# Projecting Q and K in chunks of eight heads with 26 block products

## The chip, the cores and the metric

The kernel runs on one core of a Trainium2 chip. Its time is the device time of one execution in microseconds (us); several runs are made, and their median is given. One more execution is recorded by the hardware profiler. Its instructions span a little less than its device time.

## The reference

All arithmetic is in 32-bit floats. x has 2 sequences of 512 tokens with 512 features.

```python
x = x + layernorm(attention(layernorm(x)))
x = x + layernorm(ffn(layernorm(x)))
```

The attention has 32 heads of 128, so Wq, Wk and Wv are 512 x 4096:

```python
q = rms_norm(h @ Wq + bq, gq)      # the mean square runs over all 4096
k = rms_norm(h @ Wk + bk, gk)
v = h @ Wv + bv
attn = softmax(q_head @ k_head.T / sqrt(128))
out = concat(attn @ v_head) @ Wo + bo
```

The ffn adds a base product, 512 x 512, to a gated sum of eight experts of rank 16.

## The kernel before, in words

**Stages.** The tokens of the first sequence are normalised and transposed (xTs), Q is projected, then K, then the first quarter of V. A loop over 64 pairs (head, sequence) follows, numbered i, in which scores, softmax and the weighted sum are done, with the other three quarters of V and the output projection woven in. The residual and the ffn come last.

**Projection.** `project` (line 199) goes through Q and then K in chunks of four heads (GH). Weights and tokens are split in 2 x 2 blocks and multiplied by seven block products in place of eight (Winograd's form of Strassen's scheme). For that `weight_sums` (line 188) makes four sums of weight blocks per chunk on POOL, and `token_sums` (line 177) makes four sums of token blocks once, on DVE. One block product (line 219) is, for each of two heads j, two matmuls of 128x128 weights by 128x512 tokens, added up in one PSUM bank: 28 matmuls per chunk, 16 chunks in all. DVE joins the products as they come (lines 255 to 306): one operand of nearly every join is in PSUM. ACT squares each finished head (line 240) and POOL adds the squares to accq or acck (line 241), from which the mean square comes: `ssq` for q (line 415) and `ssk` for k (line 423), both matmuls in the order of TensorE. Each head is stored in DRAM (keptq, keptk).

**Side work.** In the q stage POOL also makes the weight sums for V (`value_sums`, line 327) and DVE those for the output projection (`output_sums`, line 353); both are stored in DRAM. In the k stage DVE multiplies the stored q heads by the norm's factors: `scalings` (line 373) loads four heads at a time and stores them as keptqs, two per call of `between` (line 385).

**Value stage and head loop.** `values` (line 438) does V by the same seven products; the first 28 of its steps run ahead of the loop, each two matmuls into one of three "aux" banks. Their weights circulate in three buffers of the pool `hpool`, loaded two products ahead. `key_scales` (line 420) stands behind the third and fifth of these steps. In the loop `fetch` loads q and k three turns ahead, `scores` (line 528) multiplies them, ACT copies them out (line 535), `top_of` (line 538) takes the maximum on DVE and POOL (lines 544 to 547), DVE subtracts it (line 580), ACT takes the exponential (line 583) and TensorE multiplies by the values (line 592). Output products (line 649) are added in SBUF by DMAs that POOL issues (line 656).

**What sets the order.** TensorE (PE), VectorE (DVE), ScalarE (ACT) and GpSimd (POOL) run their instructions in the order of the program text. A framework adds the waits and gives out the buffers of each pool. SyncE (SP) issues nearly all DMAs; its order is the framework's, by when buffers come free and then by place in the text.

```python
IN_ORDER = {ET.PE, ET.DVE, ET.Activation, ET.Pool}
BANKS = (("ps", ("ps", "ps", "ps")), ("o", ("aux", "aux")), ("aux", ("ps", "aux", "aux")))
```

Of the kernel before, what the change touches and what calls it, by code (L numbers as in the profile page):

```python
# [9 lines left out]
F32 = mybir.dt.float32  # L10
# [18 lines left out]
RMS_EPS = 1e-6  # L29


@with_exitstack
def kernel(ctx: ExitStack, tc: tile.TileContext, x, wq, wk, wv, wo, vecs, rows, wbase, gates, bexp, out):
# [17 lines left out]
    npool = ctx.enter_context(tc.tile_pool(name="npool", bufs=B * NK))  # L51
    ypool = ctx.enter_context(tc.tile_pool(name="ypool", bufs=6))
    upool = ctx.enter_context(tc.tile_pool(name="upool", bufs=7))
    vpool = ctx.enter_context(tc.tile_pool(name="vpool", bufs=4))
    qpool = ctx.enter_context(tc.tile_pool(name="qpool", bufs=5))
    kpool = ctx.enter_context(tc.tile_pool(name="kpool", bufs=5))
    opool = ctx.enter_context(tc.tile_pool(name="opool", bufs=16))
    spool = ctx.enter_context(tc.tile_pool(name="spool", bufs=3))
    tmp = ctx.enter_context(tc.tile_pool(name="tmp", bufs=4))
    wpool = ctx.enter_context(tc.tile_pool(name="wpool", bufs=2))  # L60
# [8 lines left out]

    def wide(name):  # L70
        return spool.tile([P, NT, 512], F32, tag="wide", name=name)
# [17 lines left out]
    def load_w(src, name):  # L89

        w = wpool.tile([P, 4, 512], F32, tag="w", name=name)
        nc.sync.dma_start(out=w, in_=src.rearrange("(c p) f -> p c f", p=P))
        return w

# [9 lines left out]
    wq0 = load_w(wq[:, ts(0, GH * P)], "w_q0")  # L104
# [50 lines left out]
    def norm_transposed(tiles, name, tag):  # L155

        n = wide(f"n_{name}")
        pss = [pt(f"nt_{name}_{c}", tag) for c in range(NK)]
        for i, rs, shift in norms(tiles, name):
            nc.scalar.activation(n[:, i, :], tiles[i], AF.Identity, bias=shift, scale=rs)  # L160
            for c in range(NK):
                nc.tensor.transpose(pss[c][:, ts(i, P)], n[:, i, ts(c, P)], ident)

        def tiles_of():
            outs = []
            for c in range(NK):
                o = npool.tile([P, 512], F32, tag="nT", name=f"nT_{name}_{c}")
                if c % 2 == 0:
                    nc.vector.tensor_copy(o, pss[c])
                else:  # L170
                    nc.scalar.copy(o, pss[c])
                outs.append(o)
            return outs

        return tiles_of

    def token_sums(xTs):

        (b11, b21), (b12, b22) = ((xT[0:2], xT[2:4]) for xT in xTs)
        t1, t2, t3, t4 = (xpool.tile([P, 2, 512], F32, tag="x", name=f"t{i + 1}") for i in range(4))  # L180
        for c in range(2):
            nc.vector.tensor_tensor(t1[:, c], b12[c], b11[c], ALU.subtract)
            nc.vector.tensor_tensor(t2[:, c], b22[c], t1[:, c], ALU.subtract)
            nc.vector.tensor_tensor(t3[:, c], b22[c], b12[c], ALU.subtract)
            nc.vector.tensor_tensor(t4[:, c], b21[c], t2[:, c], ALU.subtract)
        return [[t[:, c] for c in range(2)] for t in (t1, t2, t3, t4)]

    def weight_sums(w, name):

        a11, a12, a21, a22 = w[:, 0:2, 0:256], w[:, 2:4, 0:256], w[:, 0:2, 256:512], w[:, 2:4, 256:512]  # L190
        pairs = [vpool.tile([P, 4, 256], F32, tag="v", name=f"s{i}_{name}") for i in range(2)]
        s1, s2, s3, s4 = out = [t[:, i : i + 2] for t in pairs for i in (0, 2)]
        nc.gpsimd.tensor_tensor(s1, a21, a22, ALU.add)
        nc.gpsimd.tensor_tensor(s2, s1, a11, ALU.subtract)
        nc.gpsimd.tensor_tensor(s3, a11, a21, ALU.subtract)
        nc.gpsimd.tensor_tensor(s4, a12, s2, ALU.subtract)
        return [a11, a12, a22] + out

    def project(xTs, sums, w_src, bias, step, name, pools, keep, accs, parts, between=lambda: None):

        G = H // GH
        begun = set()
        parts = {0: parts}
        opened = {}  # L210
        two = range(2)

        def load_next(g):
            if g < G:
                parts[g] = weight_sums(load_w(w_src[:, ts(g, GH * P)], f"w_{name}{g}"), f"{name}{g}")

        def product(g, i, a, x, j, tag=None):
            ps = pt(f"p{i}_{name}{g}_{j}", tag)
            for c in range(2):
                nc.tensor.matmul(ps, a[:, c, ts(j, P)], x[c], start=(c == 0), stop=(c == 1))  # L220
            return ps

        def column(v, g, j):
            return v[:, g * GH + j : g * GH + j + 1]

        def tile_of(what, g, j):
            return opool.tile([P, 512], F32, tag="o", name=f"{what}_{name}{g}_{j}")

        def head(g, b, j):
            pool, tag = pools[j // 2 if len(pools) > 1 else 0]  # L230
            return pool.tile([P, 512], F32, tag=tag, name=f"{name}{b}_{g * GH + j}")

        def keep_it(o, g, b, j):
            h = g * GH + j
            if b not in begun:
                begun.add(b)
                nc.scalar.activation(accs[b], o, AF.Square)
            else:
                sq = tt(f"sq_{name}{b}_{h}")
                nc.scalar.activation(sq, o, AF.Square)  # L240
                nc.gpsimd.tensor_tensor(accs[b], accs[b], sq, ALU.add)  # L241
            nc.sync.dma_start(out=keep[b, h], in_=o)

        def open_chunk(g, tag=None):
            a11, a12 = parts[g][0:2]
            ps1 = [product(g, 1, a11, xTs[0][0:2], j, tag) for j in two]
            ps2 = [product(g, 2, a12, xTs[0][2:4], j, tag) for j in two]
            u1 = opened[g] = [tile_of("u1", g, j) for j in two]

            def leave():  # L250
                for j in two:
                    nc.scalar.activation(u1[j], ps1[j], AF.Identity, bias=column(bias, g, j), scale=1.0)
                for j in two:
                    o = head(g, 0, j)
                    nc.vector.tensor_tensor(o, ps2[j], u1[j], ALU.add)
                    keep_it(o, g, 0, j)

            return leave

        if len(xTs) < B:  # L260
            load_next(1)
            leave = open_chunk(0, "ps")
            second = norm_transposed(xs[1], "a1", "aux")
            leave()
            xTs.append(second())
            leave = open_chunk(1, "ps")
            sums.extend(token_sums(xTs))
            leave()
        t1, t2, t3, t4 = sums
        for g in range(G):  # L270
            if g + 1 not in parts:
                load_next(g + 1)
            a11, a12, a22, s1, s2, s3, s4 = parts.pop(g)
            if g not in opened:
                parts[g] = (a11, a12)
                open_chunk(g)()
                del parts[g]
            u1 = opened.pop(g)
            between()
            u2 = [tile_of("u2", g, j) for j in two]  # L280
            for j in two:
                ps = product(g, 6, s2, t2, j)
                nc.vector.tensor_tensor(u2[j], ps, u1[j], ALU.add)
            between()
            u3 = [tile_of("u3", g, j) for j in two]
            for j in two:
                ps = product(g, 7, s3, t3, j)
                nc.vector.scalar_tensor_tensor(u3[j], ps, column(step, g, j), u2[j], ALU.add, ALU.add)
            between()
            for j in two:  # L290
                ps = product(g, 4, a22, t4, j)
                o = head(g, 0, j + 2)
                nc.vector.tensor_tensor(o, ps, u3[j], ALU.add)  # L293
                keep_it(o, g, 0, j + 2)
            between()
            for j in two:
                ps = product(g, 5, s1, t1, j)
                o = head(g, 1, j + 2)
                nc.vector.tensor_tensor(o, ps, u3[j], ALU.add)
                nc.vector.tensor_tensor(u2[j], ps, u2[j], ALU.add)  # L300
                keep_it(o, g, 1, j + 2)
            between()
            for j in two:
                ps = product(g, 3, s4, xTs[1][2:4], j)
                o = head(g, 1, j)
                nc.vector.tensor_tensor(o, ps, u2[j], ALU.add)
                keep_it(o, g, 1, j)
            yield g

    def attention():  # L310
# [16 lines left out]
        def value_sums(p, c):  # L327
# [10 lines left out]
            for i, w in enumerate((s1, s2, s3, s4)):  # L338
                nc.sync.dma_start(out=keptw[p, i, c], in_=w)
# [648 lines left out]
```

## Time and profile before

| what | value |
|---|---|
| median of three runs (lowest, highest) | 1307.57 us (1306.94, 1312.16) |
| the profiled execution | 1305.06 us |
| its span, first to last instruction | 1303.3 us |
| q projection's first matmul, k's, value stage's | 11.6, 205.7, 401.2 us |
| POOL's additions of squares, q and k (line 241) | 62 + 62, 81.3 + 85.5 us busy |
| scaling of q (line 385) | 64, 64.1 us busy, 1042 ns mean |
| stores of keptq, keptk, keptqs | 64 each, 256 KB, 6.4 to 6.7 us to landing |
| HBM read, written | 149.26 MB, 84.93 MB |

In the profile a group is a line of the kernel with its engine, its operation and its tiles, written out<-in; `x` counts instructions. A matmul of 32-bit floats shows as two instructions. PEld is the loading of weights, which runs beside PE. The busy time of an engine in a stretch is followed by its count; the last three numbers of such a row are the granted TensorE clock (1.00 is full), the busy share of the DMA engines and GB/s. A bracket at the end of a row tells how long the engine was idle before it and what released it.

### The profile page before, as it was taken

How to read it: one execution, taken by the hardware profiler on the slowest of the kernel's cores; microseconds unless marked ns; L12 is line 12 of the kernel's file. 1: busy time of each engine (PE TensorE's matmuls, PEld its weight loads, DVE VectorE, ACT ScalarE, POOL GpSimd, SP SyncE). 2: the span in 40 equal slices, each digit the busy share in tenths (PEclk: the TensorE clock that was granted, in tenths of full speed). 3: DMA queues.
4: the chain of work that ended last, by engine and by line, in shares of the span. 5: the costliest groups of instructions: out<-in, count | busy, mean ns of one | idle time of the engine just before them, and what ended most of it. 6: DMA issues, size and time to landing. Idle time of an engine off the chain costs nothing.

```text
span 1303.3 us, 11742 instructions
## 1 busy us (share of the span) xinstructions
PE 1279.0 (98%) x3518; PEld 652.2 (50%) x3518; DVE 977.8 (75%) x1208; ACT 541.8 (42%) x746; POOL 496.9 (38%) x382
## 2 busy tenths in 40 slices
PE   7999999999999999999999999999999999999997
PEld 4444444444444444455555555555555655555453
DVE  7565665877656468888787877778787888888976
ACT  5222222322221153445445454554545555565353
POOL 4789897555764011111121322223232232333102
PEclk9999999999999999999999999999999999999999
DMA  8789978699998765534356566566566555643301
GB/s 292 254 321 314 337 275 309 229 330 323 307 326 286 255 199 187 176 131 130 114 168 178 139 196 166 141 183 173 157 175 172 134 156 139 164 108 84 85 14 65
DMA packets 150335, 257.01 MB, mean 197 GB/s; under 512 B 12160, under 2 KB 41728, under 8 KB 150272
## 3 DMA queue, kind: packets, MB, share of 16 engines
q1 hardware_dynamic: 137312, 232.67, 52.7%
q0 software_dynamic: 12096, 22.03, 10.3%
q10 hardware_dynamic: 864, 1.57, 0.3%
q8 instruction: 28, 0.46, 0.1%
q14 instruction: 35, 0.29, 0.1%
HBM read 149.26 MB, written 84.93 MB: 180 GB/s over the span
## 4 chain that ended last, share of the span: by engine, by line
PE 68%; DVE 2%; ACT 1%; issue 0%; ACTq 0%
PE ps L534 17%; PE o L592 17%; PE aux L463 15%; PE aux L649 12%; PE psy L695 2%; PE p_k L220 2%; PE f L867 1%; PE hg L860 1%; ACT s L583 1%; PE f L923 1%; PE aux L566 0%; ACT n_f L160 0%; DVE quarters L553 0%; DVE y L830 0%; PE ssk L423 0%
## 5 line engine op out<-in xcount | busy, mean ns | idle before, releaser
L547 POOL PARTITION_ALL_REDUCE top<-m x64 | 122.2, 1910 | 606.0 <-DVE m L545 606.0
L535 ACT ACTIVATE s<-ps,rk 128x512 f32<-128x512 f32 x256 | 175.8, 687 | 308.6 <-PE ps L534 287.4
L592 PE MATMUL o<-s,v 128*128 128x512 f32 x512 | 230.6, 593 | 3.4 <-ACT s L583 3.4
L534 PE MATMUL ps<-qh,kh 128*128 128x512 f32 x512 | 230.2, 592 | 0.0
L534 PEld LDWEIGHTS ps<-qh,kh 128*128 128x128 f32 x512 | 97.3, 190 | 122.5 <-issue 120.5
L592 PEld LDWEIGHTS o<-s,v 128*128 128x128 f32 x512 | 97.0, 190 | 103.8 <-issue 95.7
L553 DVE TRANSPOSE_TENSOR_REDUCE quarters<-s 128x64 f32<-128x2048 f32 x64 | 147.2, 2300 | 0.0
L580 DVE TENSOR_TENSOR s<-s,top 128x2048 f32<-128x2048 f32 x64 | 146.0, 2282 | 0.0
L544 DVE TENSOR_TENSOR m<-s 128x1024 f32<-128x1024 f32 x64 | 78.0, 1219 | 62.0 <-ACT s L535 62.0
L583 ACT ACTIVATE s<-s 128x2048 f32<-128x2048 f32 x64 | 121.7, 1901 | 5.0 <-DVE s L580 5.0
L463 PE MATMUL aux<-w_v,t 128*128 128x512 f32 x256 | 115.8, 596 | 0.0
L649 PE MATMUL aux<-wr,oh 128*128 128x256 f32 x448 | 103.0, 380 | 0.0
L649 PEld LDWEIGHTS aux<-wr,oh 128*128 128x128 f32 x448 | 84.6, 190 | 23.2 <-issue 13.2
L241 POOL TENSOR_TENSOR accq<-accq,sq_q 128x512 f32<-128x512 f32 x62 | 81.3, 1313 | 34.6 <-ACT sq_q L240 33.0
L240 ACT ACTIVATE sq_k<-k 128x512 f32<-128x512 f32 x62 | 38.7, 630 | 133.9 <-DVE k L293 63.3
L240 ACT ACTIVATE sq_q<-q 128x512 f32<-128x512 f32 x62 | 38.9, 630 | 133.1 <-DVE q L293 68.3
L241 POOL TENSOR_TENSOR acck<-acck,sq_k 128x512 f32<-128x512 f32 x62 | 85.5, 1383 | 20.5 <-ACT sq_k L240 17.4
L463 PE MATMUL aux<-w_v,nT_a 128*128 128x512 f32 x192 | 87.5, 596 | 0.0
L220 PE MATMUL p_q<-t,s_q 128*128 128x512 f32 x192 | 85.0, 592 | 0.0
L220 PE MATMUL p_k<-t,s_k 128*128 128x512 f32 x192 | 85.0, 592 | 0.0
L649 PE MATMUL aux<-wr,s_o 128*128 128x256 f32 x336 | 77.4, 380 | 0.0
L463 PEld LDWEIGHTS aux<-w_v,t 128*128 128x128 f32 x256 | 47.6, 190 | 55.0 <-issue 54.0
(185 smaller groups left out, 1703.1 us busy)
## 6 DMA issues: line engine op xcount, KB each, us to landing
keptq<-q SPq DMA_DIRECT2D x64, 256.0 KB, 6.4
q<-keptq SPq DMA_DIRECT2D x16, 1024.0 KB, 6.6
keptk<-k SPq DMA_DIRECT2D x64, 256.0 KB, 6.6
w_v<-keptw SPq DMA_DIRECT2D x32, 512.0 KB, 4.0
keptqs<-q SPq DMA_DIRECT2D x64, 256.0 KB, 6.7
qh<-keptqs SPq DMA_DIRECT2D x64, 256.0 KB, 2.9
kh<-keptk SPq DMA_DIRECT2D x64, 256.0 KB, 2.7
keptv<-o_v SPq DMA_DIRECT2D x64, 256.0 KB, 3.0
```

The source lines that it names most:

```text
L220: nc.tensor.matmul(ps, a[:, c, ts(j, P)], x[c], start=(c == 0), stop=(c == 1))
L241: nc.gpsimd.tensor_tensor(accs[b], accs[b], sq, ALU.add)
L463: nc.tensor.matmul(ps, x[c][:, ts(t, P)], w[:, c, :], start=(c == 0), stop=(c == 1))
L534: nc.tensor.matmul(ps, kk[i][:, ts(k, P)], qs[i], start=True, stop=True)
L535: nc.scalar.activation(s[:, k, :], ps, AF.Copy, scale=rks[b][:, k : k + 1])
L544: nc.vector.tensor_tensor(m, s[:, 0:2, :], s[:, 2:4, :], ALU.max)
L547: nc.gpsimd.partition_all_reduce(ms[i], m[:, 0, :], P, ReduceOp.max)
L553: nc.vector.tensor_reduce(quarters.rearrange("p k j -> p (k j)"), ss[i].rearrange("p k (j r) -> p (k j) r", r=32), AX.X, ALU.add, apply_tr ...
L580: nc.vector.tensor_tensor(s, s, top.unsqueeze(1).to_broadcast([P, NT, 512]), ALU.subtract)
L583: nc.scalar.activation(ss[i], ss[i], AF.Exp)
L592: nc.tensor.matmul(po, vs[b, c][:, k, ts(j, P)], ss[i][:, k, :], start=(k == 0), stop=(k == NT - 1))
L649: nc.tensor.matmul(ps[:, t, :], a, right_of[i, g][:, j, :], start=(j == 0), stop=(j == 1))
```

## The change

The first two q chunks (eight heads) keep the seven products. The other 24 q heads and all k heads are done in seven chunks of eight heads. A chunk's weights are 4 x 2 blocks of 256 x 256 and the tokens 2 x 4 blocks of 256; tables written into the kernel list 26 block products (`PRODUCTS`) where two chunks of before took 14 of twice the size, 18 sums of weight blocks per chunk (`W_SUMS`), 19 sums of token blocks made once (`X_SUMS`, on DVE), and 25 joins. A product is four matmuls of 128x128 weights by 128x256 tokens. Products are added up in PSUM in eight chains of two to four products, and two stand alone: a chain's bank is copied out by ACT (`COPIES`, 16) or read by a join while the chain goes on. `JOINS` lists the 25 joins on DVE; in 15 of them both operands are in SBUF. `STEPS` gives each step a time in units of one product, and an agenda puts the steps of all chunks, side work too, in one order by these times. Of the 18 weight sums POOL makes 13 ("w") and DVE 5 ("v").

A chunk's output block is two heads by 256 tokens, so ACT adds nine biases in halves and POOL adds each square in two halves of 128x256. Seven PSUM banks circulate, an eighth is for ssq. Weights are loaded in blocks of 256 KB, eight products ahead.

Side work: the output sums 0 to 4 lie in the q chunks; the value sums of the first three quarters lie in the k chunks and are DVE's now; output sums 5 and 6 and the last value sums lie behind value steps 1 to 20, with group 6 in the two buffers of `hpool` ("h"). Of q, the heads of the first 52 turns are scaled in the loop, two turns ahead, directly in front of `top_of`, and are fetched from keptq; the last 12 are scaled in the k chunks and stored. The buffers of the q and k stage are given back at its end and used again by the later pools. The memory for DMAs that POOL issues is set to 8192.

```diff
+SCALED = 52
+PRODUCTS = (
+    (25, 21, 5, 25), (15, 2, 2, 15), (11, 9, 3, 11), (24, 18, 14, 24), (3, 16, 21, 25), (7, 11, 25, 7),
...
+STEPS = (
+    (-8.07, "w", 9), (-6.54, "w", 16), (-5.78, "w", 21), (-4.19, "v", 18), (-2.28, "w", 11), (0.0, "p", 25), (1.0, "p", 15),
+    (1.36, "c", 25), (2.0, "p", 11), (2.34, "w", 15), (2.88, "c", 15), (3.0, "p", 24), (3.23, "c", 11), (3.87, "w", 10),
...
+    (27.57, "a", 33), (27.94, "q", 47), (29.1, "a", 47), (29.58, "q", 39), (31.39, "a", 39),
+)
...
+            def product(self, k):
+                (w, x), root = operands[k], chain_of[k]
+                begun = root in self.banks
+                if not begun:
+                    self.banks[root] = free_banks.pop(0)
+                ps, a, moving = self.banks[root], self.a[w], block_of_x(x)
+                for j in range(2):
+                    for c in range(2):
+                        nc.tensor.matmul(
+                            ps[:, j, :], a[:, c, ts(j, P)], moving[:, c, :],
+                            start=(j == c == 0 and not begun), stop=(c == 1), skip_group_check=True,
+                        )
...
+            def join(self, v):
+                sign, y, z = joins[v]
...
+                nc.vector.tensor_tensor(to, y[0], z[0], ALU.add if sign > 0 else ALU.subtract)
...
+            def square(self, v):
...
+                nc.sync.dma_start(out=self.kept[n // 2, n % 2, self.h0 // 2 + i], in_=o)
+                sq = self.squared[v] = tt(f"sq_{self.name}{self.h0}_{v}").rearrange("p (j f) -> p j f", j=2)
+                nc.scalar.activation(sq, o, AF.Square)
+
+            def accumulate(self, v):
+                _, n = outputs[v]
+                acc = self.accs[n // 2][:, n % 2, :]
+                for j in range(2):
+                    nc.gpsimd.tensor_tensor(acc, acc, self.squared[v][:, j, :], ALU.add)
...
+        for n, sums_of in enumerate(X_SUMS):
+            agenda.add(-9.5 + 0.6 * n, lambda s=sums_of: x_sum(*s))
+        for g in range(5):
+            of = OutputSums(g)
+            agenda.add(16 * g - 13, of.load)
+            for n in range(4):
+                agenda.add(16 * g + 4 * n - 1.5, lambda of=of, n=n: of.step(n))
...
+        for b in range(B):
+            agenda.add(KB + 8.5 + b, lambda b=b: begin_rq(b))
...
         for n in range(28):
             next(v_steps)()
+            if n >= 1 and extra:
+                extra.pop(0)()
             if n in (2, 4):
                 key_scales(n // 2 - 1)
             if n == 12:
                 for i in range(3):
                     fetch(i)
+            if n in (16, 17):
+                scale(n - 16)
...
+            if i + 2 < N:
+                scale(i + 2)
             top_of(i + 1)
...
-    nc = bacc.Bacc("TRN2", target_bir_lowering=False, num_devices=1)
+    nc = bacc.Bacc("TRN2", target_bir_lowering=False, num_devices=1, dynamic_dma_scratch_size=8192)
```

The letters of `STEPS`: p product, c copy, j join, w and v weight sum on POOL and DVE, q bias, store and square, a addition of the square.

## Prediction

> **What bounds the kernel now.** First the page: busy shares and the chain that ended last.
>
> ```profile
> span 1303.3 us, 11742 instructions
> ...
> PE 1279.0 (98%) x3518; PEld 652.2 (50%) x3518; DVE 977.8 (75%) x1208; ACT 541.8 (42%) x746; POOL 496.9 (38%) x382
> ...
> PE 68%; DVE 2%; ACT 1%; issue 0%; ACTq 0%
> ```
>
> TensorE is never free and the chain runs over it. A share of the whole span says nothing of the stage that changes, so next the busy time by stage; the rows are the q projection, the k projection and the end of the head loop, the columns PE, PEld, DVE, ACT, POOL.
>
> ```profile
> 27.20:205.70 178.50, 178.50 (x417) 79.03 (x416) 105.74 (x138) 45.91 (x73) 151.13 (x115) 1.00 0.85 291
> 205.70:401.30 195.60, 194.80 (x455) 86.11 (x454) 141.80 (x180) 49.72 (x81) 126.16 (x92) 1.00 0.88 306
> ...
> 1010.00:1213.00 203.00, 198.93 (x619) 115.25 (x618) 177.56 (x167) 116.96 (x150) 66.34 (x55) 1.00 0.52 129
> ```
>
> PE is full at granted clock 1.00; but POOL is second in the q projection at 85% (151.13 of 178.50), and it is POOL that the change leans on. Third, prices, from the chain in order of time (start, us, piece) and from the timelines of DVE and POOL around 66 us.
>
> ```profile
> 466.64 3.43 PE ps L534 x8
> ...
> 563.67 3.45 PE aux L649 x16
> ```
>
> ```profile
> 62.81 0.81 DVE L357 TENSOR_TENSOR wo<-wo 128x512 f32<-128x512 f32 x1
> 63.66 1.64 DVE L358 TENSOR_TENSOR wo<-wo,wo 128x512 f32<-128x512 f32 x1
> 65.34 1.64 DVE L359 TENSOR_TENSOR wo<-wo,wo 128x512 f32<-128x512 f32 x1
> 67.01 1.63 DVE L360 TENSOR_TENSOR wo<-wo 128x512 f32<-128x512 f32 x1
> 68.57 1.28 DVE L255 TENSOR_TENSOR q<-p_q,u_q 128x512 f32<-128x512 f32 x2
> ```
>
> ```profile
> 57.89 8.54 POOL L241 TENSOR_TENSOR accq<-accq,sq_q 128x512 f32<-128x512 f32 x6
> 66.39 1.71 POOL L334 TENSOR_TENSOR a_v<-a_v,a_v 128x512 f32<-128x512 f32 x1
> 68.17 1.60 POOL L335 TENSOR_TENSOR s_v<-a_v,a_v 128x512 f32<-128x512 f32 x1
> 69.74 1.26 POOL L336 TENSOR_TENSOR a_v<-a_v,a_v 128x512 f32<-128x512 f32 x1
> 70.97 1.26 POOL L337 TENSOR_TENSOR a_v<-a_v,s_v 128x512 f32<-128x512 f32 x1
> ```
>
> Read: a matmul of the code is two instructions, so 512 columns cost 2 x 3.43/8 = 0.858 us and 256 columns 2 x 3.45/16 = 0.431, exactly half. A POOL addition of 128x512 steps by 1.23 us when alone (69.74 to 70.97). While DVE works on two SBUF operands the POOL steps are 1.78 and 1.57, and the DVE instruction takes 1.64 where one with a PSUM operand, beside the same busy POOL, takes 0.69 (line 283: 0.68 to 0.69). So the two slow each other, by 0.34 to 0.55 us of POOL for each such DVE instruction; I take 0.45.
>
> **Matmuls.** Removed: 6 q chunks and 8 k chunks of 28 matmuls, 392 x 0.858 = 336.1 us; they fill 62.2 to 401.3 (339.1 us) but for 1.7 of the norm's product and 1.3 idle. Added: 7 chunks of 26 x 4 = 104 matmuls of 256 columns, 728 x 0.431 = 314.0, a chunk of 44.85 us, a product 1.725. On the path: **-22 us**, if nothing else is late.
>
> **ACT**, a chunk: 16 copies (5 in two halves), 16 squares, 9 biases in two halves: 55 instructions. At the full-size step of 0.60 each, 33 us, at half of it for the halves 24; either lies beside 44.85. Off the path.
>
> **POOL**, a chunk: 13 weight sums x 1.23 = 16.0, and 32 additions of 128x256, which the trace does not show. Half of the full step is 0.61, the whole of it 1.23. In the contended stretch a POOL and a DVE instruction share 1.67 us (63.66 to 65.34), of which DVE's step is 0.60; so 1.07 is the part of POOL that scales, 0.16 fixed, and the half is 0.69. I take 0.69; 1.23 would need all cost to be fixed, against which stands a memset of 128x1 at 0.10. Sum 16.0 + 22.1 = 38.1 of 44.85, 85%.
>
> **DVE**, a chunk: 25 joins, 15 of them with both operands in SBUF (their products were copied first), 5 weight sums, and 6.7 output sums (q) or 6 value sums and 3 early scalings (k), which are all of the two-SBUF kind: 27 to 29, where the q chunks of before had 8 for eight heads. Over the stage 7 x 20 + 20 + 24 + 12 = 196, and 19 sums of x ahead: 215. Uncontended DVE has (10 + 29) x 0.6 = 23 of 44.85, contended 10 x 0.6 + 29 x 1.64 = 54. With 0.85 of them meeting POOL at work they cost POOL 215 x 0.85 x 0.45 = 82 us.
>
> POOL's queue up to the last addition of k's squares is thus 7 x 38.1 = 267, 7 for six old additions that fall in the lead, 82: 356. It starts 8.07 products (13.9 us) ahead of the first product, so it ends at 342 after it. What waits: the ssk products (line 423), which stand in PE's queue after three value steps (PE 406.32 now, 344 after the start of the stage). Net **-2 us** for the stage, in place of -22. If POOL kept up, PE would be through at 314 + 1.7, and the last addition is due 6.2 products (10.6 us) after the last product: ssk at 326, **-18**; behind it all value products wait. If all 215 collide at 0.55, POOL needs 378: **+34**. These are the ends.
>
> [...]
>
> **Start.** The sixth product needs the 17th sum of x, due 5 products (8.6 us) after the start, DVE starting 16.4 ahead: 17 x 0.6 to 1.64 = 10 to 28, with 8 exits x 0.6 and three other sums 17 to 38 in 25 us: 0 to +13, I take +2 as POOL has gaps there.
>
> **Value steps.** The sums for output group 6 move behind value step 11 and use two of the three "h" buffers in which value weights circulate. The two loads stand ahead of the weights for step 16 in order of priority; these then get a buffer only as step 15 ends, and land 4.0 us after issue ("w_v<-keptw", DMA issues), so PE waits about 4; the weights of step 18 find one buffer free and wait 4 again: **+8** (0 if the loads are ordered behind, 12 at 6 us each). The first value exits stand behind the last chunk's squares on ACT, which end about 5.7 us after the last product when uncontended; three banks cover 5.2: 0.5, inside the wait for ssk. The new sums on DVE (16 x 0.6 to 1.6) lie beside 54 us in which DVE works 24.
>
> **Head loop.** 50 scalings of 0.74 us (line 385, uncontended median 0.744) move to DVE's queue ahead of the maximum. DVE has 201 of 253 us in 757 to 1010, and waits 3.6 to 4.1 there for scores: nothing. From 1010 on:
>
> ```profile
> 1041.99 1.22 DVE L544 TENSOR_TENSOR m<-s 128x1024 f32<-128x1024 f32 x1
> ...
> 1046.37 2.28 DVE L580 TENSOR_TENSOR s<-s,top 128x2048 f32<-128x2048 f32 x1
> 1050.02 1.22 DVE L544 TENSOR_TENSOR m<-s 128x1024 f32<-128x1024 f32 x1 [1.38 <-ACT s L535]
> ```
>
> One scaling fits in the 1.38; the other pushes the subtraction's end from 1048.65 to 1049.4, and the exponential starts at 1049.89 anyway. Six heads fall here before the early-scaled ones: +0.5, at most 6 x 0.74 = 4.4. What waits behind it is the maximum, then POOL and exponentials. Gone are the k stage's 64 scalings with their 64 stores and 16 loads of 1 MB: DMA at 0.88 falls, which no wait of PE pays for. The 1 KB pieces in which heads are now fetched land three heads (30 us) ahead against 2.9 us: nothing. The memory for POOL's own DMAs is halved; the trace does not show its filling. POOL issues one or two of them per head of 10 us or more and they land in 4.5 us, so I take 0; a wait for one landing would hold the next maximum by up to 4.5 us, of which 1.2 (1048.65 to 1049.89) is covered.
>
> **Sum.** -2 + 2 + 8 + 0.5 = +8.5 on 1303.3; with 1.8 outside the span 1313.6 against the profiled 1305.06. The median of the runs is 1307.57, 2.5 above that one: **1316**.
>
> **Rivals.** *PE stays the bound* (POOL's halves at 0.61, few collisions as it has gaps): -18 + 1 + 8 = -9, 1298; without the buffer stall 1290. For it: POOL at 85% ran beside a full PE in the q stage; against: there DVE sent it 4 colliding instructions per 24 us, now 27 per 45. It decides as soon as POOL's chunk is under 44.85, i.e. fewer than 15 collisions per chunk. *POOL and DVE hold each other* (all collide, joins at 1.64 free the banks late): 215 x 0.45 makes POOL 357, +13, with 12 + 5 + 3 around it +33: 1340. For it: 54 us of contended DVE work; against: ten joins and the gaps. *The change does less than it says*: the first two q chunks keep the 28 matmuls, as counted, and 256-column matmuls might not sustain 0.2156 behind a 190 ns weight load; the 16-instruction pieces do, so I give this no time.
>
> **Chances.** 0.52 for the POOL-bound case (1303 to 1330, its middle 1316), 0.28 for PE-bound (1288 to 1299), 0.20 for the mutual hold (1325 to 1345). A measurement here tells 0.5% from no change, 1301 and 1314: faster 0.31 (the second case and a little of the first), slower 0.51 (three fifths of the first, all of the third), same 0.18. Range 1288 to 1338, leaving out the tails of the outer cases.
>
> **What would show it.** POOL-bound: POOL over 95% busy between the first product and the value stage, PE waits there released by POOL's weight sums, POOL's joint step above 1.5 us, the ssk product released by the last addition, one or two 4 us gaps of PE on "w_v" DMAs after value step 15. PE-bound: products back to back at 44.9 us a chunk. Wrong altogether: chunks above 53 us released by DVE joins or ACT copies, or a head loop that grows by more than 5 us.

## The result, and the profile after

The change made the kernel slower: 1353.17 us (median of four runs, 1353.01 to 1354.55) against 1307.26 us for the kernel before, run beside it. The ratio is 1.0349, 95% interval 1.0318 to 1.0381. The forecast was 1316 us in a range of 1288 to 1338: the direction is right, the size is not, by 37 us.

The page of the changed kernel, the lines that answer to those shown of before:

```profile
span 1351.4 us, 13585 instructions
...
PE 1279.1 (95%) x4190; PEld 786.7 (58%) x4190; DVE 1087.8 (80%) x1275; ACT 643.8 (48%) x991; POOL 587.8 (43%) x501
...
POOL 4579999999999001111112222232222233323102
...
PE 72%; POOL 17%; DVE 5%; issue 3%; ACT 2%; DMA 1%; SPq 0%; ACTq 0%; POOLq 0%; DVEq 0%
```

TensorE is as long busy as before (1279 us), but 48 us more go by. POOL is full in one block of slices, which is the products' stage, and holds 17% of the chain that ended last, where before it did not appear. Busy time by stage (products; start of the value stage; 14 us in it; columns as before, then granted clock, DMA share, GB/s):

```profile
67.00:435.00 368.00, 333.87 (x1461) 280.76 (x1459) 287.50 (x287) 193.08 (x391) 349.27 (x313) 0.98 0.57 195
435.00:500.00 65.00, 51.41 (x115) 23.67 (x116) 29.37 (x46) 5.05 (x10) 5.94 (x7) 0.84 0.83 284
470.00:484.00 14.00, 7.93 (x11) 3.08 (x12) 4.02 (x6) 0.00 (x0) 0.00 (x0) 0.62 0.97 341
```

POOL is 95% busy in the first stretch (349.27 of 368.00). In the second TensorE, never free before, is busy for 51 of 65 us at granted clock 0.84. Where TensorE waited (total, times, longest), first in the products' stage, then in the value stage:

```profile
PE bank L413 <- ACT u_k L430: 8.7, 4, 3.3
PE bank L413 <- POOL ws_k L403: 7.9, 7, 3.3
PE bank L413 <- ACT u_q L430: 7.9, 3, 3.0
PE bank L413 <- POOL ws_q L403: 4.3, 4, 2.5
```

```profile
PE aux L733 <- DMA w_v<-keptw: 6.1, 1, 6.1
PE ssk L693 <- POOL acck L470: 5.7, 2, 5.2
PE aux L733 <- DMA w_v<-in_wv: 4.1, 1, 4.1
```

Three causes: POOL's weight sums come late, banks are copied out late by ACT (which waits in its own order for DVE's joins; these are stretched beside POOL, to 1.21 us in the median with two SBUF operands, and in DVE's order stand weight sums that wait 57.2 us for POOL's), and the value stage waits for POOL's last addition and for two loads. What such a wait costs beside its own length is read in TensorE's timeline of the value stage (start, us, instructions, idle before):

```profile
437.94 1.01 PE L693 MATMUL ssk<-ones,acck 128*128 128x1 f32 x4 [5.21 <-POOL acck L470]
...
440.30 3.76 PE L733 MATMUL aux<-w_v,nT_a 128*128 128x512 f32 x4
443.86 2.03 PE L733 MATMUL aux<-w_v,t 128*128 128x512 f32 x4
...
469.77 6.20 PE L733 MATMUL aux<-w_v,nT_a 128*128 128x512 f32 x8 [4.11 <-DMA w_v<-in_wv]
482.04 3.48 PE L733 MATMUL aux<-w_v,t 128*128 128x512 f32 x4 [6.07 <-DMA w_v<-keptw]
```

Before, the same view has for eight and for four such instructions:

```profile
433.86 1.88 PE L463 MATMUL aux<-w_v,t 128*128 128x512 f32 x4
435.58 3.60 PE L534 MATMUL ps<-qh,kh 128*128 128x512 f32 x8
```

After each wait they take up to twice that: 1.9 + 0.1 + 2.6 + 1.6 = 6.2 us more in these four rows.

The span's +48.1 us (1303.3 to 1351.4), by the first instruction of each stage:

| stretch | before | after | difference |
|---|---|---|---|
| start to the first of the products that changed | 62.2 | 64.4 | +2.2 |
| products, to the first value product | 339.0 | 363.0 | +24.0 |
| first value product to first scores | 34.4 | 57.9 | +23.5 |
| first scores to the end | 867.7 | 866.1 | -1.6 |

In the products' stage 31.7 us are TensorE waits, where the 22 us fewer matmuls (314.0 + 1.7 us of the norm's product) should have left it at 316; of the remaining 15.6 us the lowered clock has 8.5: in five stretches of 3.4 us, from 338.4 to 341.7 us for one, the granted clock was 0.50. The other 7 us are in short gaps and are not resolved further. In the value stage it is 15.9 of waits, and 7.7 by which TensorE is busy longer (42.09 us against 34.40), 6.2 of them the four rows above.

What the additions on POOL and the joins cost each other (line, engine, output<-inputs, count: shortest/median/longest ns):

```profile
L470 POOL TENSOR_TENSOR acck<-acck,sq_k x128: 721/1056/1249, 246.4 to 438.6; 128x256 f32<-128x256 f32 x128
```

```profile
L447 DVE TENSOR_TENSOR k<-u_k,u_k x44: 621/1208/1764, 241.5 to 429.2; 128x512 f32<-128x512 f32 x44
L447 DVE TENSOR_TENSOR k<-u_k,bank x8: 673/675/689, 249.3 to 423.1; 128x512 f32<-128x512 f32 x8
```

A half addition left alone takes 0.72, in the median 1.06. A join with both operands in SBUF takes 1.21 in the median, one with an operand in PSUM 0.67 to 0.69.

### The profile page after: what moved, and what is told of

It is laid out like the page before. It is cut to its first block, busy times and chain, and to the rows that moved or that the text cites. A ratio compares the mean times of both kernels' runs of the same rounds, so it can differ in the third digit from the quotient of the medians.

```text
span 1351.4 us, 13585 instructions
## 1 busy us (share of the span) xinstructions
PE 1279.1 (95%) x4190; PEld 786.7 (58%) x4190; DVE 1087.8 (80%) x1275; ACT 643.8 (48%) x991; POOL 587.8 (43%) x501
## 4 chain that ended last, share of the span: by engine, by line
PE 72%; POOL 17%; DVE 5%; issue 3%; ACT 2%; DMA 1%; SPq 0%; ACTq 0%; POOLq 0%; DVEq 0%
PE ps L812 16%; PE o L870 16%; PE aux L733 14%; PE aux L927 12%; POOL acck L470 6%; PE bank L413 5%; POOL accq L470 4%; POOL ws_k L403 4%; PE p_q L569 3%; POOL ws_q L403 2%; PE psy L973 2%; PE f L1160 1%; DVE xs L358 1%; PE hg L1153 1%; ACT s L861 1%
## 5 line engine op out<-in xcount | busy, mean ns | idle before, releaser
L470 POOL TENSOR_TENSOR acck<-acck,sq_k 128x256 f32<-128x256 f32 x128 | 123.2, 972 | 7.0 <-ACT sq_k L464 1.6
L413 PE MATMUL bank<-xs,ws_k 128*128 128x256 f32 x416 | 102.4, 397 | 16.7 <-ACT u_k L430 8.7
L822 DVE TENSOR_TENSOR m<-s 128x1024 f32<-128x1024 f32 x64 | 78.1, 1220 | 37.8 <-ACT s L813 37.6
L413 PEld LDWEIGHTS bank<-xs,ws_k 128*128 128x128 f32 x416 | 81.6, 198 | 33.4 <-POOL ws_k L403 10.7
L733 PE MATMUL aux<-w_v,nT_a 128*128 128x512 f32 x192 | 92.0, 621 | 4.1 <-DMA w_v<-in_wv 4.1
L470 POOL TENSOR_TENSOR accq<-accq,sq_q 128x256 f32<-128x256 f32 x96 | 89.9, 946 | 8.7 <-ACT sq_q L464 4.7
L413 PE MATMUL bank<-xs,ws_q 128*128 128x256 f32 x312 | 76.1, 395 | 13.0 <-ACT u_q L430 7.9
L933 ACT COPY w<-aux 128x512 f32<-128x512 f32 x84 | 47.9, 582 | 59.3 <-PE aux L927 50.3
```

What stands on the lines that cost most here:

```text
L413: nc.tensor.matmul(ps[:, j, :], a[:, c, ts(j, P)], moving[:, c, :], start=(j == c == 0 and not begun), stop=(c == 1), skip_group_check=True,)
L470: nc.gpsimd.tensor_tensor(acc, acc, self.squared[v][:, j, :], ALU.add)
L733: nc.tensor.matmul(ps, x[:, c, ts(t, P)], w[:, c, :], start=(c == 0), stop=(c == 1))
```

## The experiments

Two theories on the products. *POOL's queue*: the two-SBUF work of DVE and the additions of POOL stretch each other until POOL's queue sets the pace, and all later waits hang on it. *TensorE's own feed*: the small products, the eight chains in seven banks and ACT's copies are what is late, and POOL is only busy beside them. On the value stage: *buffers* (the step of the forecast: the two "h" buffers that the output sums take) against *traffic* (the loads and stores that were moved there).

Every run below but the last was executed once. The kernel before, executed beside them, took 1305.9 to 1307.5 us, but 1304.3 to 1311.2 in the eleven executions beside the last run; a difference of a few us between two single runs therefore rests on the stages of their traces more than on their times.

**The buffers.** Group 6 of the output sums gets a tile of its own.

```diff
-                self.of = halves_of(self.g)
+                if self.g == 6:
+                    w = tools["wide"]("halves6")
+                    self.of = [w[:, 2 * k : 2 * k + 2, :] for k in range(2)]
```

> The sums of output group 6 are made in a free 8 KB buffer of the score pool in place of the two buffers in which the value weights circulate. If the two waits of TensorE in the value steps (4.1 and 6.1 us, released by w_v DMAs) come from these buffers, both go, and with them the lowered clock behind them (about 3 us): 1353 falls to about 1340. If the DMA queue or HBM is late for another reason, the waits stay and the time stays within 2 us of 1353.

Measured 1353.85 us. TensorE's timeline at the same place:

```profile
470.10 6.16 PE L737 MATMUL aux<-w_v,nT_a 128*128 128x512 f32 x8 [4.45 <-DMA w_v<-in_wv]
479.80 3.75 PE L737 MATMUL aux<-w_v,t 128*128 128x512 f32 x4 [3.54 <-DMA w_v<-keptw]
```

The waits stay, 8.0 us in place of 10.2. In the changed kernel the step of the forecast is there to see: the first of the two loads is issued at 465.69, just as the value step that held its buffer ends, and lands after 3.95 us. With the buffers free it is issued 2.5 us earlier, and TensorE gets on no sooner. First the two loads in the changed kernel (start, us from issue to landing), then the first one's issue here:

```profile
465.69 3.95 DMA w_v<-in_wv
476.01 5.90 DMA w_v<-keptw
```

```profile
463.19 0.48 SPq L721 DMA_DIRECT2D w_v<-in_wv  x1
```

The loads take longer now: from 460 to 485 us the "w_v<-in_wv" loads land after 7.7 us (median of two), where the changed kernel's page has 4.2 for such loads; the DMA engines are full (1.06 in the row of 470 to 484). So the buffers are a cause, but not the only one: with them free, the loads are held up nearly as long beside full DMA engines.

**Without the additions.** All half additions of squares on POOL go.

```diff
-                    nc.gpsimd.tensor_tensor(acc, acc, self.squared[v][:, j, :], ALU.add)
+                    pass
```

> POOL's 224 additions of squares in the seven chunks are left out, so the norms of q and k are wrong; the squares themselves are still made. Theory 1, POOL's queue is the bound: it loses 210 of its 361 us, the products run back to back, 363 us from the first product to the value stage become 316 to 325, the wait for ssk goes, 1353 falls to 1295 to 1305. Theory 2, the joins (1.2 us where two SBUF operands meet POOL) free the banks late and POOL only follows: the stage stays above 345 and the time above 1335. Theory 3, products of 256 columns don't keep their rate: the stage stays near 363.

Measured 1302.58 us, 50.6 less. The products' stage and the waits of TensorE in it and behind it:

```profile
64.40:386.40 322.00, 316.68 (x1461) 277.56 (x1460) 224.53 (x290) 189.47 (x382) 128.51 (x94) 1.00 0.66 219
```

```profile
PE aux L733 <- DMA w_v<-keptw: 5.2, 1, 5.2
PE aux L733 <- DMA w_v<-in_wv: 4.9, 1, 4.9
PE bank L413 <- ACT u_q L430: 3.0, 1, 3.0
PE bank L413 <- DVE u_q L447: 2.4, 1, 2.4
```

322.0 against 363.0, and 1302.58 us as forecast for POOL's queue (1295 to 1305): without POOL's additions the same products, chains, copies and joins keep TensorE fed at clock 1.00, six us above what the matmuls need. The waits for ACT were an effect of POOL too (16.6 to 3.0). This rules out the feed theory as the main cause. The two DMA waits are not touched.

**The joins out of SBUF.** The 15 joins per chunk that read two SBUF operands take their first one from a spare PSUM bank; all counts are kept.

```diff
+                if all(k not in chain_of or k in copies for _, k in (y, z)):
+                    y = (spare[0], y[1])
```

> Each of the 15 joins per chunk with two SBUF operands reads the eighth PSUM bank in place of its first operand, so q and k are wrong; instruction counts and sizes stay. Theory 1 with collisions: 105 of 216 colliding instructions are gone, POOL's half additions fall from 0.94 towards 0.70 and its work from 361 to about 315, time 1310 to 1325. If the half additions are slow by themselves, POOL stays at 350 or more and the time above 1340. Theory 2 (joins free banks late): joins at 0.68 in place of 1.2 bring 1310 too, but with POOL's step unchanged.

Measured 1311.02 us, the stage 327.6. The stage's busy times, then the additions and the joins of k:

```profile
64.94:392.51 327.57, 321.05 (x1462) 278.76 (x1461) 230.35 (x291) 187.18 (x382) 305.80 (x309) 0.99 0.64 215
```

```profile
L472 POOL TENSOR_TENSOR acck<-acck,sq_k x128: 717/730/1232, 228.7 to 398.9; 128x256 f32<-128x256 f32 x128
```

```profile
L449 DVE TENSOR_TENSOR k<-bank,u_k x52: 621/678/692, 227.1 to 392.8; 128x512 f32<-128x512 f32 x52
```

The median addition falls from 1.06 to 0.73 with all its work still there. POOL does the same work in 306 us of the stage where it took 342 before, and the stage is 35 us shorter, of the 41 that leaving the additions out gave. DVE's weight sums still wait 58.9 us for POOL's, so these waits are not what costs. So it is not POOL's work in itself, but that work meeting DVE instructions with two SBUF operands.

**Half the additions' instructions.** One addition of 128x512 per square, which the code allows if the two heads of a square have tiles of their own that ones-matmuls add up later; POOL has 104 additions, not 224.

```diff
-                for j in range(2):
-                    nc.gpsimd.tensor_tensor(acc, acc, self.squared[v][:, j, :], ALU.add)
+                if v in self.squared:
+                    nc.gpsimd.tensor_tensor(acc, acc, self.squared[v], ALU.add)
```

> The squares are added with one POOL instruction of 128x512 each in place of two of 128x256, into one sum for each quarter of tokens that keeps the two heads apart; the norm's product on TensorE adds them up (6 small matmuls more for q, 8 for k). Theory 1 with a cost per colliding DVE instruction: additions 108 x 1.23 = 133 in place of 154 plus the same 82 of collisions, POOL 361 to about 338, time about 1328. Theory 1 with a cost per POOL instruction (each waits for DVE once): 112 instructions fewer at 0.25 to 0.3 in addition, about 1305. Theory 2: unchanged, 1345 or more.

Measured 1340.85 us, a gain of 12 only; none of the three prices fits. POOL is at 85% now:

```profile
64.00:413.40 349.40, 326.04 (x1478) 278.40 (x1477) 312.81 (x287) 185.21 (x377) 296.63 (x191) 1.00 0.60 201
```

```profile
PE bank L415 <- DVE u_k L449: 6.4, 4, 2.9
PE bank L415 <- ACT u_k L432: 5.1, 4, 2.5
```

Who waits has changed: TensorE waits for joins and copies, and for POOL's weight sums only 1.6 us. DVE is busy for 312.81 of 349.40 with 287 instructions, where before this edit as many took 287.50 of 368.00. Its two-SBUF joins are stretched more than before, to 1.39 in the median, against 1.21:

```profile
L449 DVE TENSOR_TENSOR k<-u_k,u_k x44: 621/1394/1759, 229.6 to 416.7; 128x512 f32<-128x512 f32 x44
```

As far as the waits show, POOL, relieved, hands the bound to DVE.

**Moving the weight sums to DVE.** On top of the edit above, POOL's 13 weight sums per chunk go to DVE, which had 5 of them already.

```diff
-                        "w": lambda v=v: self.weight_sum(v, nc.gpsimd),
+                        "w": lambda v=v: self.weight_sum(v, nc.vector),
```

> Wide additions (POOL 16 per chunk), and all 18 weight sums on DVE. Theory: POOL and DVE take turns for two-SBUF work, about 1.07 us for a POOL instruction and 0.6 for DVE's; the sum of both decides. It was 52 us a chunk with wide additions (29 x 1.07 + 27 x 0.6 = 47, and waiting for each other's order), over the 44.9 of the products; now 16 x 1.07 + 40 x 0.6 = 41, under it. The products from first to last then need 318 to 330 us in place of 349, time 1305 to 1320. Rival: DVE itself is the bound (10 + 40 instructions of 0.6 are 30, with each of the 40 waiting 0.5 are 50): stage above 345, time above 1335.

Measured 1322.59 us, a little above what the theory of turns gave (1305 to 1320) and below its rival; the stage is 332.6:

```profile
63.70:396.30 332.60, 321.86 (x1477) 279.52 (x1476) 313.67 (x374) 186.47 (x377) 160.85 (x103) 1.00 0.63 211
```

DVE does 87 instructions more in the same busy time (313.67 against 312.81): what it no longer loses to POOL (the joins' median is 0.69 here) pays for all of them.

**The side work in the value stage.** In the changed kernel as it is, output sums 5 and 6 and the last value sums go into the q and k chunks, whose side work is set closer.

```diff
-        for g in range(5):
+        for g in range(7):
...
-            agenda.add(16 * g - 13, of.load)
+            agenda.add(11 * g - 13, of.load)
...
-        for m in range(6):
+        for m in range(8):
...
-            agenda.add(KB + 16 * m - 4, of.load)
+            agenda.add(KB + 11.5 * m - 4, of.load)
```

> Output sums 5 and 6 and the last value sums are made in the q and k chunks (seven groups 11 products apart, eight value halves 11.5 apart), not behind value steps 1 to 20. If the two waits in the value steps come from the DMA traffic of this side work (freeing the buffers alone did not end them), both go: the value stage is 34 to 36 us from its first product to the first scores, if ssk's wait stays 40 to 44, in place of 58. POOL's queue gets 16 more collisions of 0.45, 7 us. Net: 1353 to 1343 to 1348. If the waits have another cause, 1353 to 1360.

Measured 1345.27 us. Both DMA waits are gone, and from the first value product to the first scores it is 43.9 us in place of 57.9; the wait for ssk stays (5.9), and the products' stage grows from 363.0 to 369.4. This run takes the side work's buffers and its traffic out of the value stage together; freeing the buffers alone had left the waits. A run with the traffic gone and the buffers still held was not made. Beside a full POOL, 6 of the 14 us are paid in the chunks.

**Both together, and the additions instead of the sums.** First the sums on DVE with the side work moved; then a variant with the wide additions on DVE and the 13 sums left on POOL.

> e6 and the moved side work of e5 together. If both theories hold: products 320 to 332, value stage 35, time 1292 to 1305. If DVE is the bound, the 16 more instructions cost 10 to 15 us and eat the gain: above 1320.

> Wide additions on DVE in place of POOL, POOL keeps 13 weight sums, side work moved. By turns: 13 x 1.07 + 45 x 0.6 = 41 a chunk, as e7, so within 8 us of e7. If DVE's own queue is the bound, this one is slower than e7 by the difference in its instructions (55 against 52 per chunk, about 2 us a chunk, 14 in all).

Measured 1310.47 and 1319.51 us, stages 338.2 and 350.9; each lies between its two prices. In the second POOL is busy for only 138 us of the stage but TensorE waits longer, 15.1 us for ACT's copies alone (first: 8.5). Sums on DVE is the better half to move; the runs do not show why in more detail.

**How to share out what is left.** Three runs on the version with sums on DVE: output sums moved, last value sums left in the value stage, the two `key_scales` behind value steps 7 and 9; then all 64 turns of q scaled in the loop; then four of the weight sums of each chunk given back to POOL.

```diff
-            if n in (2, 4):
-                key_scales(n // 2 - 1)
+            if n in (6, 8):
+                key_scales(n // 2 - 3)
```

```diff
-SCALED = 52
+SCALED = 64
```

```diff
-                        "w": lambda v=v: self.weight_sum(v, nc.vector),
+                        "w": lambda v=v: self.weight_sum(v, nc.gpsimd if v in (13, 14, 17, 19) else nc.vector),
```

> e7, but only the output sums are all in the q chunks; the value sums keep their distance of 16 products in the k chunks, where e7 at 11.5 let DVE wait about 20 us for stores and loads of their buffers, and the last two value halves come back behind value steps 1 to 16, with nothing in the buffers of the value weights. The ssk products stand behind value steps 7 and 9 in place of 3 and 5. By the theory of turns the k chunks lose 10 to 15 us, ssk's 4 us go, and half of the side traffic in the value stage costs 0 to 5: 1310 to 1292 to 1300. If the traffic, not the buffers, made the waits of 5 us, up to 1303. Rival, DVE is full anyway: 1305 or more.

> e9, with all 64 heads of q scaled in the loop. DVE loses 12 instructions of 1.2 us in the k chunks and gets 12 of 0.74 in the tight end of the loop, where it waits 1.4 us in every second head. If DVE and its turns with POOL bound the k chunks: 5 to 12 us faster than e9 there, and 0 to 4 us slower in the loop. If the products bound them: no gain, 0 to 4 slower.

> e10, with 4 of the 18 weight sums on POOL again, which then works 20 x 1.07 + 36 x 0.6 = 43 us of turns a chunk in place of 41. If DVE's own length is the bound, 7 x 4 x 0.6 to 1.2 of DVE's time: 5 to 15 us faster than e10. If the common turns are: 5 to 15 slower, or no change while both are under 44.9.

Measured 1317.20, 1310.17 and 1318.13 us; stages 334.7, 330.7 and 339.6. The first is a miss, and as it changes three things at once it does not tell which of them cost; half a move keeps half of the DMA waits (3.9 and 1.7 us). The second gains 7.0 us, 4.0 of them in the products' stage. The last against the one before it is the sharpest row on the collision:

```profile
64.19:394.89 330.70, 322.53 (x1477) 280.94 (x1476) 308.72 (x372) 188.39 (x380) 162.43 (x104) 0.99 0.63 207
```

```profile
64.56:404.14 339.58, 325.83 (x1478) 281.62 (x1476) 310.12 (x350) 188.01 (x380) 189.35 (x125) 0.99 0.60 201
```

DVE has 22 instructions fewer and is busy 1.4 us longer, POOL has 21 more and is at 56%: no engine is relieved, and the stage is 8.9 us longer. In the mean a DVE instruction of the stage takes 0.89 us, where it took 0.83 (310.12/350 and 308.72/372; 0.84 if the latter is freed of 22 weight sums at 0.68). More work on an engine that is half idle costs time here, since what DVE does beside it is stretched.

**All of it.** The sums on DVE, the wide additions, all side work in the chunks, all scalings in the loop, `key_scales` later: the last edits above in one kernel.

> As e7_sums_on_dve_moved (one addition of 128x512 per square on POOL, all weight sums on DVE, all output and value sums in the q and k chunks), but all 64 turns of q scaled in the head loop and the two key_scales moved behind value steps 7 and 9, as in e10_all_scaled_in_loop. POOL-queue theory (what the change loses, it loses by POOL's work and by the side work that it pushed into the value steps; with both mended it is level with the kernel before or a little ahead): no twelve scalings and no keptqs loads in the k chunks, so the products' stage is between e10's 330.7 us and e7's 338; first value product to first scores as in e7, 39.5; scores to end 867: 64.5 + 334 + 39.5 + 867 = 1305 in the span, 1302 to 1309 by the two ends of the stage, time 1304 to 1311, the same as before within 0.5%. Rival (the side work only moves its collisions: put into the chunks it costs there what it saves behind them, DVE being 92% busy): the stage is over 340 and the time over 1311.

Measured 1300.11 us (median of six, 1298.98 to 1300.94) against 1305.58 for the kernel before on the same chip: ratio 0.9953, interval 0.9936 to 0.9970. That is faster than both kernels, though than the first by half a per cent only, and better than was expected of it (1304 to 1311). The products' stage, then what TensorE waited for from there to the first scores:

```profile
63.83:393.42 329.59, 321.11 (x1477) 279.78 (x1476) 309.01 (x380) 188.55 (x381) 164.77 (x104) 1.00 0.67 221
```

```profile
PE bank L415 <- ACT u_q L432: 2.9, 2, 2.3
PE bank L415 <- ACT u_k L432: 2.8, 2, 1.8
PE bank L415 <- DVE ws_q L405: 2.5, 1, 2.5
PE aux L744 <- ACT u_v L757: 1.1, 1, 1.1
PE bank L415 <- DVE k L449: 0.3, 1, 0.3
```

9.6 us of waits, where the changed kernel had 47.6; the stage is 9.4 below that of before, the value stage 37.6 us against 34.4. The weight sums, now DVE's, run undisturbed in the median, though the longest still take 1.76:

```profile
L405 DVE TENSOR_TENSOR ws_k<-w_k,w_k x24: 677/679/1757, 193.6 to 364.3; 128x512 f32<-128x512 f32 x24
```

## Why the prediction was right in direction and wrong in size

The forecast was +8.5 us in the span; measured are +48.1. Point by point:

- **Matmuls, -22: right.** Without the additions the stage is 322.0, 17 below before, with 5.4 us of waits still in it.
- **POOL's work, 356 us: right to 6; "so it ends at 342 after it": this step failed.** POOL worked for 362 us, but its last addition ended at 439.4, 375 after the first product. From its first weight sum (50.2) to that end it was idle for 27.5 us, a term that the sum had at nothing. 15.1 of them are four waits ahead of 91.1 us, for squares of the last old chunk and for the first square of the new chunks:

```profile
59.08 3.19 POOL L590 TENSOR_TENSOR accq<-accq,sq_q 128x512 f32<-128x512 f32 x2 [5.79 <-ACT sq_q L589]
66.50 2.96 POOL L590 TENSOR_TENSOR accq<-accq,sq_q 128x512 f32<-128x512 f32 x2 [2.55 <-ACT sq_q L589]
73.20 3.13 POOL L590 TENSOR_TENSOR accq<-accq,sq_q 128x512 f32<-128x512 f32 x2 [2.07 <-ACT sq_q L589]
91.07 6.20 POOL L470 TENSOR_TENSOR accq<-accq,sq_q 128x256 f32<-128x256 f32 x6 [4.69 <-ACT sq_q L464]
```

ACT had waited for DVE's joins ahead of each of these squares (9.5, 6.2, 4.8 and 5.4 us), and DVE was busy for 39.9 of the 40.8 us from 50.2 to 91.0, with sums of x of up to 1.75 us in its order. So more than the lead of 13.9 us, which the sum counted in full, went in waits. Another 10.8 us are gaps of less than 0.1 us between POOL's instructions. Behind 91.1 us POOL waited for squares for 1.6 us only: there it was simply full, 336 of 348 us, and set the chunks at 51.9 us, where its forecast work, 38.1 + 82/7, is 49.8.
- **"Net -2 for the stage": failed with it.** From the first product to ssk it was 373.5 us, 29.4 more than before; 31 of the 40 us that were missed lie here.
- **The price of the collision, 0.45 each: about right,** as POOL's work came out. A half addition lost 0.34 in the median (1.06 against 0.72), a join 0.53 (1.21 against 0.68); DVE's two-SBUF instructions took about 1.21 beside a half addition (the join that starts at 253.03) and 1.75 beside a weight sum (the one at 303.72).
- **ACT "off the path": wrong in part.** Its 33 us lie beside 44.85, but 16.6 us of TensorE's waits end at its copies. They are POOL's lateness passed on, as leaving the additions out showed (3.0).
- **Value steps, +8 by buffers: cost nearly right, cause not the whole.** The two waits came, 4.1 and 6.1 us, at the weights of steps that I had named, and the first load was issued and landed as forecast. But freeing the buffers left 8.0 of them, for then the traffic held the loads up nearly as long; the sum had no term for it. Not in the sum either were the slowed matmuls behind the waits (6.2).
- **Start, +2: right** (+2.2), but POOL's waits in the lead were missed. **Head loop, +0.5: nothing of weight** there, as forecast (-1.6 from the first scores on; 52 scalings at 0.743 in the median).
- **The signs that the forecast named** showed in the main: POOL at 95%, TensorE released by weight sums (12.2 us, though 16.6 by ACT's copies), weight sums of POOL at 1.49 to 1.72 in the median, ssk released by the last addition, two DMA waits. I gave the mutual hold 0.20 and priced it at 1340; it was the case nearest to the result, and even its price lacked POOL's idle time and the lowered clock.

On the clock: at and behind the first DMA wait of the value stage the granted clock was 0.50 from 468.1 to 474.8 us.

```profile
468.10:474.80 6.70, 5.03 (x6) 2.19 (x7) 2.46 (x4) 0.00 (x0) 0.00 (x0) 0.50 0.99 332
```

The matmuls began at 469.77, so they ran for 5.0 us at half clock. At the other two waits of that stage it was the same: 0.50 from 437.3 to 444.1 us at the one for ssk, and from 478.3 to 485.0 at the second load. The five stretches of 3.4 us in the products' stage begin 0.3 to 1.1 us behind waits of 2.0 to 3.4 us, at 75.5, 177.9, 229.1, 338.4 and 386.1 us. What sets their lengths was not shown.

What stays open: what the 7 us of short gaps in the products' stage are, why the version with the additions on DVE loses to the one with the sums there, and whether the last 5.7 us of waits for ACT's copies could be taken away by another order.

## What to carry to other kernels

Before work is added to an engine that is 85% busy, count how often it will meet its neighbour's instructions of the kind that stretch it (a half addition took 1.06 us here in the median, 0.72 left alone). Do not take a queue's end from the sum of its work: ask what it waits for at its start, and add the gaps between its instructions. The sum here was right to 6 us and the end wrong by 33. A cheaper main loop is worth nothing until its helpers have slack; here the better half was to take work off POOL, even though DVE was 90% busy and ended at 94%. Where loads had been moved into a stretch whose DMA engines were full (0.97 and 1.06), the loads that were there landed late (after 7.7 us with their buffers free, 4.2 in the median of the changed kernel), and a cause that is taken away can uncover a second one of the same size.

## What the runs showed of the hardware that was not expected

- POOL's 128x256 addition took 0.72 us alone against 1.26 for 128x512, so half the size cost 57%; the estimate of 0.69 held. In the changed kernel it takes 1.06 in the median, and 0.73 when the joins read PSUM.
- Moving work to a half-idle POOL did not relieve DVE: taking 22 instructions off DVE and putting 21 on a half-idle POOL left DVE's busy time where it was (308.7 and 310.1 us).
- In the value stage a wait of TensorE cost more than its length: the four groups of matmuls behind 15.4 us of waits took 6.2 us longer than such groups before.
